# A four-layer residual kernel: where the first batch's weight splits sit, with four raw tiles and nine ring places in place of two and ten

## The chip, the cores and the metric

The kernel runs on one core of one Trainium2 chip. Its time is the device time of one execution in microseconds (us); the figure for a kernel is the median of its runs.

## The reference

Sixteen batches of a 256 x 256 input go through four residual layers, each `x = x + layer(x)`.

- Layer 0: a causal moving average along the sequence, a gate from `x` and that average, then 16 further gated moving averages ("traces"), mixed with per-batch weights, a second gate, a projection and a layer norm.
- Layer 1: `p = softmax(mask + v . tanh(x W1 + b1))` over 256 positions, then `pooled = p x / count`.
- Layer 2: eight experts and one shared expert, each `(silu(x Wg) * (x Wu)) Wd` with hidden width 1024, added up with per-batch gate values. All nine sets of weights are used for every batch.
- Layer 3: `gelu(x W1 + b1)` of width 1024, then an output of 192 shared columns and 64 columns whose weights each batch picks from eight sets.

```python
g = einsum('bsd,edf->ebsf', h, Wg); u = einsum('bsd,edf->ebsf', h, Wu)
expert_outs = einsum('ebsf,efd->ebsd', silu(g) * u, Wd)
expert_output = einsum('be,ebsd->bsd', gating_probs, expert_outs)
```

## The kernel before

**Split operands.** Every big matmul is done three times: a float32 operand is split into a rounded high part (`rnd`, line 89, ScalarE) and a low part, the rest (`low`, line 96, a subtraction on VectorE or GpSimd), and `mm3` (lines 102 to 104) adds up high x high, high x low and low x high. Batch 0 alone takes layers 0 and 1 in plain float32 (`first_traces`, `first_pooled`), without splits.

**Weights.** Layer 2 has 72 weight pieces, here called chunks, of 128 x 768 floats, and `load_chunk` brings one in: a DMA from HBM into a raw tile (`raws`, two buffers), `rnd` on ScalarE into the high half of a ring tile (`ring`, `RING = 10` places), and `low` on GpSimd or VectorE into the other half. A raw tile is free again when `low` has read it; a ring place when TensorE has done the last matmul with the chunk. On the second visit the split chunk is stored in HBM (`keep`), and from then on it is loaded ready-made straight into its ring place, without a raw tile. Layer 3 has eight chunks `w_f` and four `w_c` for each pair of batches, in the same ring. `prefetch(n)` issues the next n chunks of a fixed list; behind each work item as many are issued as chunks are done with.

**Order of the work.** Layer 2 is a list of units. `l2_unit` makes up to 512 columns of `pg` and `pu`, `hidden` makes `silu(pg) * pu` and splits it (`hh`), and `down` multiplies by `Wd` into `y`, two units later (`LAG = 2`). For the first five experts (`ALONE`) batch 0 rides alone: 20 units of two chunks each. From unit 21 on batches 0 and 1 ride together, one chunk to a unit; further pairs join later (batches 2 and 3 at unit 57). In between, the steps of layers 0 and 1 of the next batches (`traces(b)`, `pooled(b)`) are dealt out by `pace`, so that a batch is ready when it boards. `issue_after(ins)` puts the instructions of a block that run on the engine of `ins` behind it in that engine's queue, and does nothing to those on other engines. Within these limits a scheduler decides the order on every engine, and each engine runs its queue strictly in order.

**What the change touches.** The small weights of layers 0 and 1 (`small_a`, `small_b`) are split by `split_small` into `wh` and `wl`: three pieces behind the first batch's traces, and four (`rest`) at steps 1, 6, 9 and 12 of batch 1's traces in program order. Eight chunks of the first expert are prefetched around the first batch: which engine takes their low part is decided in `load_chunk`:

```python
if kind == "e" and key[1] == 0:
    e = "g" if key[2] < 2 else "v" if key[2] < 6 else "gv"[key[2] % 2]
elif kind == "e" and key[1] < ALONE and key[2] % 3 == 0:
    e = "g"
```

In `first_pooled`, `evict(c, ...)` copies PSUM tiles to SBUF, on ScalarE for `c = 0` and on VectorE otherwise.

Of the kernel before, what the change touches and what calls it, by code (L numbers as in the profile page):

```python
# [11 lines left out]
AF = mybir.ActivationFunctionType  # L12
ALU = mybir.AluOpType
# [4 lines left out]
S = 256  # L18
# [1 line left out]
ND = 16  # L20
NE = 8
NF = 8
RING = 10
FRONT = 4
FRONT0 = 3
SLACK = 16
# [8 lines left out]
FIRST = 13  # L35
# [4 lines left out]
O_N1, O_G, O_SO, O_TE, O_OU, O_W1, W_COLS = 0, 256, 1280, 1792, 2304, 2816, 3072  # L40

V_BG, V_BN1, V_BN2, V_BSO, V_BTE, V_B1, V_V, V_L3B1, V_B2, V_WN2, V_COLS = 0, 2, 3, 4, 6, 8, 9, 10, 18, 19, 67
# [3 lines left out]
def fused_kernel(  # L46
# [21 lines left out]
    V, G, A, PE = nc.vector, nc.gpsimd, nc.scalar, nc.tensor  # L68
# [2 lines left out]
    xin = ctx.enter_context(tc.tile_pool(name="xin", bufs=2))  # L71
    l0 = ctx.enter_context(tc.tile_pool(name="l0", bufs=1))
    ring = ctx.enter_context(tc.tile_pool(name="ring", bufs=RING))
    raws = ctx.enter_context(tc.tile_pool(name="raws", bufs=2))
    xs = ctx.enter_context(tc.tile_pool(name="xs", bufs=3))
    accp = ctx.enter_context(tc.tile_pool(name="accp", bufs=3))
    hp = ctx.enter_context(tc.tile_pool(name="hp", bufs=2))
# [7 lines left out]
    last_of = {}  # L85
# [51 lines left out]
    def split_small(c0, n, e):  # L137
        rnd("a", wh[:, c0 : c0 + n], small(c0, n))
        low(e, wl[:, c0 : c0 + n], small(c0, n), wh[:, c0 : c0 + n])
# [6 lines left out]
    vec = const([P, V_COLS], F32, "vec", vecs)  # L146
# [42 lines left out]
    mhalf = cp.tile([P, 2], F32, name="mhalf")  # L189
# [69 lines left out]
    rest = {1: (O_SO, 512), 6: (O_TE, 512), 9: (O_OU, 512), 12: (O_W1, 256)}  # L259

    def traces(b):

        xr = xin_tiles.pop(b)
        xh, xl = hl(f"x_{b}", "hA")
        rnd("a", xh, xr)
        low("g", xl, xr, xh)
        cx = ft("ta", f"ctx{b}")
        for c in range(2):
            V.tensor_tensor_scan(
                cx[:, c], decay[:, ND : ND + 1].to_broadcast([P, S]), xr[:, c], 0.0, ALU.mult, ALU.add  # L270
            )
        yield
        ch, cl = hl(f"c_{b}", "hA")
        rnd("a", ch, cx)
        low("v", cl, cx, ch)

        ph = ps_l.tile([P, 512], F32, tag="ps", name=f"ph{b}")
        for k in range(2):
            o = O_N1 + k * P
            mm3(ph[:, :S], W(0, o, P), W(1, o, P), xh[:, k], xl[:, k], k == 0, k == 1)  # L280
        hg = l0.tile([P, S], F32, tag="hg", name=f"hg{b}")
        A.activation(hg, ph[:, :S], AF.Gelu, bias=vec[:, V_BN1 : V_BN1 + 1])
        hs = l0.tile([P, S], F32R, tag="hs", name=f"hs{b}")
        rnd("a", hs, hg)
        low("v", hs[64:], hg[64:], hs[64:])
        yield
        pm = ps_l.tile([P, 512], F32, tag="ps", name=f"pm{b}")
        PE.matmul(pm[:48, :S], n2[:, 0], hs, start=True, stop=False)
        PE.matmul(pm[:48, :S], n2[:, 1], hs, start=False, stop=True)
        md = l0.tile([48, S], F32, tag="md", name=f"md{b}")  # L290
        A.activation(md, pm[:48, :S], AF.Tanh, bias=hb[:48, V_BN2 : V_BN2 + 1], scale=0.5)
        V.tensor_scalar(md, md, 0.5, 1.0, ALU.mult, ALU.add)
        mdd = dram.tile([1, ND, S], F32, tag="mdd", name=f"mdd{b}")
        nc.sync.dma_start(mdd[0], md[0:ND])
        yield
        pg = ps_l.tile([P, 2, S], F32, tag="ps", name=f"pg{b}")

        ga = ps_a.tile([P, 2, S], F32, tag="ga", name=f"gp{b}")
        for m in range(2):
            for k in range(4):  # L300
                o = O_G + k * S + m * P
                xa, xb_ = (xh[:, k], xl[:, k]) if k < 2 else (ch[:, k - 2], cl[:, k - 2])
                mm3(pg[:, m], W(0, o, P), W(1, o, P), xa, xb_, k == 0, k == 3)
        for m in range(2):
            A.activation(ga[:, m], pg[:, m], AF.Tanh, bias=hb[:, V_BG + m : V_BG + m + 1], scale=0.5)
        V.scalar_tensor_tensor(ga, ga, 1.0, xr, ALU.add, ALU.mult)
        yield
        sm = ft("sm", f"sm{b}")

        def soma():  # L310
            pso = ps_l.tile([P, 2, S], F32, tag="ps", name=f"pso{b}")
            for m in range(2):
                for k in range(2):
                    o = O_SO + k * S + m * P
                    mm3(pso[:, m], W(0, o, P), W(1, o, P), xh[:, k], xl[:, k], k == 0, k == 1)
            for m in range(2):
                A.activation(sm[:, m], pso[:, m], AF.Gelu, bias=vec[:, V_BSO + m : V_BSO + m + 1])

        tacc = ft("ta", f"ta{b}")
        for d in range(ND):  # L320
            if d % 2 == 0:
                mod = l0.tile([P, 2, S], F32, tag="mod", name=f"mod{b}_{d}", bufs=2)
                nc.sync.dma_start(mod, mdd[0, d : d + 2].partition_broadcast(P))
            bt = ft("bt", f"bt{b}_{d}", 3)
            tr = tacc if d == 0 else ft("tr", f"tr{b}_{d}", 3)
            with tc.issue_after(last_of[0].ins) if b == 1 and "h" not in last_of else nullcontext():
                for c in range(2):
                    V.scalar_tensor_tensor(
                        bt[:, c], ga[:, c], bl[:, c, d : d + 1], mod[:, d % 2], ALU.mult, ALU.mult
                    )  # L330
            for c in range(2):
                V.tensor_tensor_scan(  # L332
                    tr[:, c], decay[:, d : d + 1].to_broadcast([P, S]), bt[:, c], 0.0, ALU.mult, ALU.add
                )
            if d:
                G.tensor_tensor(tacc, tacc, tr, ALU.add)  # L336
            if b == 1 and d in rest:
                split_small(*rest[d], "g")
            if d == 5:
                soma()  # L340
            yield
        th, tl = hl(f"t_{b}", "hA")
        rnd("a", th, tacc)
        low("v", tl, tacc, th)
        xt = xt_tiles.pop(b)
        G.tensor_tensor(xt, xt, bet.unsqueeze(1).to_broadcast([P, 2, S]), ALU.add)
        held[b] = xt, sm, th, tl
        yield
# [122 lines left out]
    def evict(c, o, i):  # L471

        if c == 0:
            last_of["ca"] = A.activation(o, i, AF.Copy)
        else:
            last_of["cv"] = V.tensor_copy(o, i)
# [83 lines left out]
    def first_pooled():  # L560
# [19 lines left out]
        rs = l0.tile([P, 2], F32, tag="rs", name="rs0")  # L580
# [5 lines left out]
            V.bn_stats(st[:, t], po[t])  # L586
            V.bn_aggr(mv[:, t], st[:, t])
        V.tensor_scalar(rs, mv[:, :, 1], 4e-5, None, ALU.add)
        G.tensor_tensor(rs, rs, mhalf, ALU.pow)
        for t in range(2):  # L590
            V.scalar_tensor_tensor(po[t], po[t], mv[:, t, 0:1], gam, ALU.subtract, ALU.mult)
        yield
# [6 lines left out]
        ptr = two("ptr0")  # L599
# [2 lines left out]
                PE.transpose(ptr[c][:, t * P : (t + 1) * P], x1[:, t, c * P : (c + 1) * P], ident)  # L602
        x1T = ft("xo", "x1T0")
        for c in range(2):
            evict(c, x1T[:, c], ptr[c])
        yield
        pa = ps_l.tile([P, 512], F32, tag="ps", name="pa0")
        for k in range(2):
            PE.matmul(pa[:, :S], small(O_W1 + k * P, P), x1T[:, k], start=k == 0, stop=k == 1)
        ta = l0.tile([P, S], F32, tag="th", name="th0")  # L610
        last_of["ca"] = A.activation(ta, pa[:, :S], AF.Tanh, bias=vec[:, V_B1 : V_B1 + 1])
        yield
        psc = ps_l.tile([P, 512], F32, tag="ps", name="psc0")
        PE.matmul(psc[:, :S], vec[0:64, V_V : V_V + 1].to_broadcast([64, P]), ta[0:64], start=True, stop=True)
# [12 lines left out]
        for j in range(2):  # L627
            js = slice(j, j + 1)
            V.tensor_tensor(sums[:, js], sums[:, js], cntb[:, 0, js], ALU.mult)
            V.reciprocal(sums[:, js], sums[:, js])  # L630
            last_of["cv"] = V.tensor_scalar(sc[:, j], sc[:, j], sums[:, js], None, ALU.mult)
        yield
        ppt = two("ppt0")
        for l in range(2):
# [1 line left out]
                PE.transpose(ppt[l][:, j * P : (j + 1) * P], sc[:, j, l * P : (l + 1) * P], ident)  # L636
        q = ft("bt", "q0", 3)
        for l in range(2):
            evict(l, q[:, l], ppt[l])
        yield  # L640
        pp = two("pp0")
        for l in range(2):
# [17 lines left out]
    def load_chunk(key):  # L660
# [10 lines left out]
        if kind == "e":  # L671
            n = 768
# [14 lines left out]
        e = "v"  # L687
        if kind == "e" and key[1] == 0:

            e = "g" if key[2] < 2 else "v" if key[2] < 6 else "gv"[key[2] % 2]  # L690
        elif kind == "e" and key[1] < ALONE and key[2] % 3 == 0:
            e = "g"
        low(e, t[:, 1, :n], raw[:, :n], t[:, 0, :n])
# [181 lines left out]
    def prefetch(n, boost=BOOST):  # L875
        while n > 0 and nxt[0] < len(order):
            k = order[nxt[0]]
            if k[0] == "c" and k[1] not in eregs:
                eregs[k[1]] = nc.sync.value_load(eix[0:1, k[1] : k[1] + 1], min_val=0, max_val=NE - 1)
            with tc.high_priority(offset=boost) if boost else nullcontext():  # L880
                load_chunk(k)
            nxt[0] += 1
            n -= 1
# [61 lines left out]
            with tc.issue_after(last_of["cx"].ins):  # L945
                later_constants()
    with tc.issue_after(last_of["a"].ins), tc.issue_after(last_of["g"].ins), tc.issue_after(last_of["tr"].ins):
        for off, n in ((O_N1, 256), (O_G, 512), (O_G + 512, 512)):
            split_small(off, n, "g")
        prefetch(2, 0)  # L950


    n = 2
    while n_done[0] < 1:
        with tc.issue_after(last_of["ca"].ins), tc.issue_after(last_of["cv"].ins):
            next(steps)
            if n_steps[0] > FIRST + 5 and n < 6 and n_steps[0] % 2:
                prefetch(1, 0)
                n += 1
    with tc.issue_after(last_of["ca"].ins), tc.issue_after(last_of["cv"].ins):  # L960
        coefs()
        prefetch(RING - n)
# [155 lines left out]
```

## Time and profile before

| what | value |
|---|---|
| median of 3 runs (lowest to highest) | 2840.18 us (2839.82 to 2841.34) |
| profiled execution: its own time / its span | 2841.92 us / 2840.2 us |
| mean granted TensorE clock of it | 0.994 |
| TensorE matmul busy / VectorE / ScalarE / GpSimd | 98% / 50% / 43% / 46% |
| HBM read / written | 304.62 MB / 64.21 MB, 130 GB/s |

In the profile PE is TensorE's matmuls, PEld its weight loads, DVE VectorE, ACT ScalarE, POOL GpSimd, and SP the queue that issues nearly all DMAs. Durations of matmuls are modelled and overlap, so a busy PE is not one at its peak; counts of matmuls say more. Where two numbers stand at the front of a line of the timeline, they are its start and its length in us.

### The profile page before, as it was taken

The page shows a single profiled execution, that of the slowest core. Times are in us where ns is not written, and L with a number is a line of the kernel's source. Part 1 is how long each engine was busy: PE and PEld are TensorE (multiplying, and loading weights), DVE is VectorE, ACT ScalarE, POOL GpSimd, SP SyncE. Part 2 cuts the span into 40 slices and gives each one's busy share as a digit, 9 for nine tenths or more (in the row PEclk, how much of TensorE's full clock was granted, in tenths as well). Part 3 has the DMA queues.
Part 4 walks back from the last instruction along what each step waited for, and adds up shares of the span by engine and source line. Part 5 has one row for each costly group of instructions (what it writes and reads, how often), then busy time and mean ns, then how long its engine had stood idle before and what let it go on. Part 6 is the DMA issues. An engine that isn't in the chain of part 4 may idle for free. (4 is left out here: it accounts for less than half of the span.)

```text
span 2840.2 us, 36878 instructions
## 1 busy us (share of the span) xinstructions
PE 2779.2 (98%) x13604; PEld 2335.0 (82%) x13604; DVE 1425.2 (50%) x2646; ACT 1235.4 (43%) x2043; POOL 1299.0 (46%) x986
## 2 busy tenths in 40 slices
PE   7889989999999999999999999999999999999998
PEld 4877779888888888888888888888888888888887
DVE  7888766665665364544545445453444542222222
ACT  5555544546444533435334443334433453323433
POOL 5764654544544353544534445444444443333333
PEclk9999999999999999999999999999999999999999
DMA  4444645546443533324433153331523242222552
GB/s 125 136 148 122 196 162 181 185 131 230 148 164 117 180 115 104 119 77 135 150 110 106 40 180 112 111 117 58 177 101 112 91 169 90 89 89 76 192 198 83
DMA packets 114693, 371.23 MB, mean 131 GB/s; under 512 B 12642, under 2 KB 30930, under 8 KB 114514
## 3 DMA queue, kind: packets, MB, share of 16 engines
q1 hardware_dynamic: 114082, 368.82, 39.2%
q8 instruction: 108, 1.77, 0.3%
q14 instruction: 71, 0.58, 0.1%
q10 hardware_dynamic: 432, 0.06, 0.0%
HBM read 304.62 MB, written 64.21 MB: 130 GB/s over the span
## 5 line engine op out<-in xcount | busy, mean ns | idle before, releaser
L96 POOL TENSOR_TENSOR hh<-h,hh 128x512 fp32r<-128x512 f32 x640 | 848.7, 1326 | 1317.4 <-ACT hh L89 1297.4
L745 DVE TENSOR_TENSOR h<-h,pu 128x512 f32<-128x512 f32 x576 | 393.5, 683 | 941.9 <-PE pu L104 813.0
L89 ACT ACTIVATE hh<-h 128x512 fp32r<-128x512 f32 x640 | 403.4, 631 | 936.0 <-DVE h L745 914.9
L744 ACT ACTIVATE h<-pg 128x512 f32<-128x512 f32 x576 | 342.8, 595 | 317.7 <-PE pg L104 236.5
L102 PE MATMUL pg<-x,w_e 128*128 128x512 f32 (+1 forms) x1232 | 466.3, 379 | 10.1 <-ACT h L744 3.9
L102 PE MATMUL pu<-x,w_e 128*128 128x512 f32 (+1 forms) x1232 | 464.9, 377 | 7.5 <-ACT h L744 7.4
L104 PE MATMUL pg<-x,w_e 128*128 128x512 f32 (+1 forms) x1232 | 465.3, 378 | 1.8 <-DVE w_e L96 1.4
L103 PE MATMUL y<-hh,w_e 128*128 128x512 f32 (+1 forms) x1232 | 463.7, 377 | 2.5 <-POOL hh L96 2.5
L103 PE MATMUL pg<-x,w_e 128*128 128x512 f32 (+1 forms) x1232 | 464.7, 377 | 0.8 <-POOL x L96 0.8
L103 PE MATMUL pu<-x,w_e 128*128 128x512 f32 (+1 forms) x1232 | 463.7, 376 | 0.0
L104 PE MATMUL pu<-x,w_e 128*128 128x512 f32 (+1 forms) x1232 | 463.7, 376 | 0.0
L104 PE MATMUL y<-hh,w_e 128*128 128x512 f32 (+1 forms) x1232 | 463.1, 376 | 0.0
L102 PE MATMUL y<-hh,w_e 128*128 128x512 f32 (+1 forms) x1232 | 415.2, 377 | 2.9 <-ACT hh L89 1.6
L336 POOL TENSOR_TENSOR ta<-ta,tr 128x512 f32<-128x512 f32 x225 | 308.9, 1373 | 84.4 <-DVE tr L332 72.1
L332 DVE TENSOR_TENSOR_SCAN tr<-decay,bt 128x256 f32<-128x256 f32 x450 | 284.7, 669 | 0.0
L102 PEld LDWEIGHTS pg<-x,w_e 128*128 128x128 f32 x1232 | 232.5, 189 | 53.1 <-ACT h L744 4.8
L102 PEld LDWEIGHTS pu<-x,w_e 128*128 128x128 f32 x1232 | 232.6, 189 | 51.2 <-ACT h L744 9.9
L103 PEld LDWEIGHTS y<-hh,w_e 128*128 128x128 f32 x1232 | 232.8, 189 | 46.3 <-POOL hh L96 4.6
L104 PEld LDWEIGHTS pg<-x,w_e 128*128 128x128 f32 x1232 | 232.7, 189 | 44.9 <-DVE w_e L96 2.4
L102 PEld LDWEIGHTS y<-hh,w_e 128*128 128x128 f32 x1232 | 231.5, 189 | 45.7 <-ACT hh L89 2.6
L104 PEld LDWEIGHTS y<-hh,w_e 128*128 128x128 f32 x1232 | 232.7, 189 | 41.8
L104 PEld LDWEIGHTS pu<-x,w_e 128*128 128x128 f32 x1232 | 232.5, 189 | 41.9
(279 smaller groups left out, 3220.8 us busy)
## 6 DMA issues: line engine op xcount, KB each, us to landing
w_e<-keep_e SPq DMA_DIRECT2D x216, 768.0 KB, 4.4
raw_e<-in_wexp_dram SPq DMA_DIRECT2D x144, 384.0 KB, 4.3
keep_e<-w_e SPq DMA_DIRECT2D x72, 768.0 KB, 4.3
mod<-mdd SPq DMA_DIRECT2D x120, 256.0 KB, 3.7
w_f<-keep_f SPq DMA_DIRECT2D x56, 384.0 KB, 3.5
raw_c<-in_comb_dram SPq DMA_DIRECT2D x32, 260.0 KB, 2.8
xr<-in_xT_dram SPq DMA_DIRECT2D x16, 256.0 KB, 3.7
xt<-in_x_dram SPq DMA_DIRECT2D x16, 256.0 KB, 2.7
```

Source lines behind the costliest of these rows:

```text
L89: last_of["ca"] = A.activation(out_, in_, AF.Copy)
L96: i = (V if e == "v" else G).tensor_tensor(out_, in_, h.bitcast(F32), ALU.subtract)
L102: PE.matmul(o, wh, xh, start=start, stop=False, **kw)
L103: PE.matmul(o, wh, xl, start=False, stop=False, **kw)
L104: last_of["pe"] = PE.matmul(o, wl, xh, start=False, stop=stop, **kw)
L332: V.tensor_tensor_scan(tr[:, c], decay[:, d : d + 1].to_broadcast([P, S]), bt[:, c], 0.0, ALU.mult, ALU.add)
L336: G.tensor_tensor(tacc, tacc, tr, ALU.add)
L744: A.activation(h, ps_g, AF.Silu)
L745: last_of["h"] = V.tensor_tensor(h, h, ps_u, ALU.mult)
```

## The change

- `raws` has four buffers, and `RING` is 9.
- Prefetches around the first batch are tied to other instructions: chunks 0 and 1 of the first expert are issued between the pieces of the small weights, 2 and 3 behind the `rs` power of `first_pooled` on GpSimd and the last ScalarE step, 4 behind its tanh, 5 behind its softmax division; the rest, three and not four, after the batch.
- The low parts of the first six chunks go to engines v, g, g, g, v, v (before: g, g, v, v, v, v), where v is VectorE and g GpSimd.
- `x1T` and `q` of `first_pooled` are copied from PSUM by ScalarE alone.
- The four `rest` splits of the small weights stand in an `issue_after` block on the low part of batch 0's `x2`.

```diff
-RING = 10
+RING = 9
-    raws = ctx.enter_context(tc.tile_pool(name="raws", bufs=2))
+    raws = ctx.enter_context(tc.tile_pool(name="raws", bufs=4))
...
             if b == 1 and d in rest:
-                split_small(*rest[d], "g")
+                with tc.issue_after(last_of[0].ins):
+                    split_small(*rest[d], "g")
...
-        G.tensor_tensor(rs, rs, mhalf, ALU.pow)
+        last_of["rs"] = G.tensor_tensor(rs, rs, mhalf, ALU.pow)
...
-            evict(c, x1T[:, c], ptr[c])
+            evict(0, x1T[:, c], ptr[c])
...
-            evict(l, q[:, l], ppt[l])
+            evict(0, q[:, l], ppt[l])
...
-            e = "g" if key[2] < 2 else "v" if key[2] < 6 else "gv"[key[2] % 2]
+            e = "vgggvv"[key[2]] if key[2] < 6 else "gv"[key[2] % 2]
...
-        for off, n in ((O_N1, 256), (O_G, 512), (O_G + 512, 512)):
+        prefetch(1, 0)
+        split_small(O_N1, 256, "g")
+        prefetch(1, 0)
+        for off, n in ((O_G, 512), (O_G + 512, 512)):
             split_small(off, n, "g")
-        prefetch(2, 0)
...
             next(steps)
-            if n_steps[0] > FIRST + 5 and n < 6 and n_steps[0] % 2:
+        if n == 2 and "rs" in last_of:
+            with tc.issue_after(last_of["rs"].ins), tc.issue_after(last_of["ca"].ins):
+                prefetch(2, 0)
+            n += 2
+        if n == 4 and "th" in last_of:
+            with tc.issue_after(last_of["th"].ins):
                 prefetch(1, 0)
-                n += 1
+            n += 1
+        if n == 5 and "sc" in last_of:
+            with tc.issue_after(last_of["sc"].ins), tc.issue_after(last_of["ca"].ins):
+                prefetch(1, 0)
+            n += 1
```

More of the change, by code (lines that the diff above doesn't have):

```diff
@@ L610, in first_pooled @@
         ta = l0.tile([P, S], F32, tag="th", name="th0")
-        last_of["ca"] = A.activation(ta, pa[:, :S], AF.Tanh, bias=vec[:, V_B1 : V_B1 + 1])
+        last_of["ca"] = last_of["th"] = A.activation(ta, pa[:, :S], AF.Tanh, bias=vec[:, V_B1 : V_B1 + 1])
         yield
@@ L630, in first_pooled @@
             V.reciprocal(sums[:, js], sums[:, js])
-            last_of["cv"] = V.tensor_scalar(sc[:, j], sc[:, j], sums[:, js], None, ALU.mult)
+            last_of["cv"] = last_of["sc"] = V.tensor_scalar(sc[:, j], sc[:, j], sums[:, js], None, ALU.mult)
         yield
```

## The prediction, made before the changed kernel was run

> **What bounds the kernel now.** I read the page's busy rows first, then the stretches of the first 400 us, then who waited for whom there, then single instructions.
>
> ```profile
> span 2840.2 us, 36878 instructions
> PE 2779.2 (98%) x13604; PEld 2335.0 (82%) x13604; DVE 1425.2 (50%) x2646; ACT 1235.4 (43%) x2043; POOL 1299.0 (46%) x986
> ```
>
> TensorE is the bound. Its count of matmuls does not change (the built kernel's queues hold the same matmuls), so only lost time can move. A run of 256-column matmuls starts one every 0.118 us (60 to 80 us: 169 in 20 us), 512-column ones every 0.213 us (1000 to 1500 us: 2352 in 500 us, no idle time). From 1000 to 2000 us nothing is to be had. The stretches before are another matter:
>
> ```profile
> core 0: us, PE busy (x) PEld busy (x) DVE busy (x) ACT busy (x) POOL busy (x), PEclk, DMA share, GB/s
> 78.00:101.00 23.00, 19.56 (x144) 18.65 (x143) 23.00 (x42) 10.19 (x16) 17.74 (x12) 0.93 0.49 153
> 101.00:122.00 21.00, 17.62 (x122) 16.04 (x121) 16.95 (x29) 9.29 (x14) 20.69 (x14) 0.93 0.42 132
> 122.00:150.00 28.00, 26.10 (x211) 25.45 (x211) 22.44 (x31) 21.02 (x35) 18.28 (x13) 0.99 0.45 132
> 150.00:187.00 37.00, 28.82 (x220) 26.66 (x220) 26.32 (x48) 22.17 (x36) 15.98 (x11) 1.00 0.51 157
> 187.00:388.00 201.00, 182.86 (x920) 152.63 (x921) 160.51 (x284) 107.47 (x175) 107.62 (x76) 0.96 0.47 146
> ```
>
> From 78 to 187 us, batch 0 riding alone, there are 697 matmuls, 82 us of work in 109 us: 27 us are lost. From 78 to 122 us VectorE and then GpSimd is full (batch 1's traces); from 122 to 187 us no engine is. There the weights are late:
>
> ```profile
> ACT w_e L89 <- DMA raw_e<-in_wexp_dram: 28.5, 22, 4.1
> PEld pu L102 <- ACT h L744: 6.2, 5, 2.0
> PE pu L102 <- ACT h L744: 5.2, 4, 1.8
> PE pg L102 <- ACT w_e L89: 3.1, 2, 2.1
> ```
>
> ScalarE stood 28.5 us before roundings whose raw tile had not landed, and what is queued behind them (`h`, `hh`) stood too. One turn of one of the two raw tiles, in order of time:
>
> ```profile
> 118.67 1.09 DVE L96 TENSOR_TENSOR w_e<-raw_e,w_e 128x768 fp32r<-128x768 f32 x1 [2.24 <-ACT w_e L89]
> ...
> 124.04 0.83 ACT L89 ACTIVATE w_e<-raw_e 128x768 fp32r<-128x768 f32 x1
> ...
> 125.65 2.31 POOL L96 TENSOR_TENSOR w_e<-raw_e,w_e 128x768 fp32r<-128x768 f32 x1
> ```
>
> The low part that ends at 119.76 us frees the tile, the next DMA is issued at 119.78, its rounding runs at 124.04, its low part ends at 127.96, and at 127.99 comes the DMA after it: 8.2 us for one chunk through one of two tiles. Over 77.9 to 181.0 us 32 chunks were issued, one per 3.3 us; a unit needs two per 36 matmuls (4.25 us). So two raw tiles pace this part.
>
> **The change, part by part.** *First batch (36 to 59 us): 0, from -0.5 to +0.5.* `x1T`'s second half leaves VectorE, where it began at 47.81 behind three other operations though its matmuls ended at 46.35; ScalarE, no longer rounding chunk 3 there (0.83 us from 46.25), can do both halves by 47.2, up to 0.5 us before `pa` reads the second now. But chunk 4's rounding now follows the tanh, and its low part (0.96) stands on VectorE ahead of the `mx` reductions: the tanh from 49.0, 0.47 long, then 0.83 and 0.96, is 51.3, and `mx` begins at 51.33 now. The gain is spent. The low parts of chunks 2 and 3 on GpSimd (1.85 each, against 0.95) lie where it was idle (44.94 to 48.71), and their matmuls come at 59 us or later. The DMAs of chunks 2 and 3 (41.18 now) can go at about 15 us, ahead of nothing urgent on SP's queue.
>
> A low part on VectorE takes 0.95 us when GpSimd is still and up to 2.11 us when both run (60.78 us). The Trainium skill ("SBUF — State Buffer", "SBUF: two separate sides") says why: GpSimd and a VectorE operation with two SBUF inputs share a port pair, and the later one waits for the whole instruction. That speaks against the move to GpSimd; by it the low part of `c` could wait until 48.7 us for chunk 3's, and the term would still be 0, since `mx` waits for chunk 4.
>
> *The `rest` splits: 0.* The instruction they are tied to is VectorE's, the splits run on ScalarE and GpSimd, and in the built kernel's queues they stand where they stood (9.09 to 13.7 us on GpSimd). This part does not do what it says.
>
> *Four raw tiles, batch 0 alone (59 to 187 us): -3.0, from -8.8 to +4.* The new queue order shows what the scheduler makes of it. Counted from unit 1's first matmul (58.9 us), batch 1's `pt`, which needs the end of its traces, stands behind 496 matmuls, not 438; `psc` behind 788, not 660; unit 21 behind 852, not 840. Units run ahead of batch 1, and its last steps, spread over units 17 to 20 now, come in one piece after them. So:
> - `pt` starts at 124.66 now. The traces end on a GpSimd that is full, and one more `hh` (1.3) and one more low part (1.85) stand before that end: 124.7 + 3.2 = 127.9.
> - From `pt` to `psc` 292 matmuls: 34.5 us at 0.118, 39.9 at the 0.1365 of that stretch now (222 in 30.3 us, 124.66 to 154.96). I take the middle, 37.1, since the weights come sooner but a ring place comes later: 165.0.
> - From `psc` to unit 21 the serial piece. Batch 3 shows its price today:
>
> ```profile
> 369.05 0.38 PE L420 MATMUL psc<-ths,vr 128*128 128x256 f32 x1 [0.56 <-ACT md L291]
> 372.24 1.16 PE L445 MATMUL ppt<-ident,sc 128*128 128x128 f32 x4 [2.69 <-DVE sc L437]
> 375.30 0.55 PE L102 MATMUL pg<-x,wh 128*128 128x256 f32 x1 [1.90 <-DVE q L96]
> 380.89 0.38 PE L457 MATMUL pp<-q,v 128*128 128x256 f32 x1 [1.02 <-ACT gp L305]
> 385.34 0.50 PE L102 MATMUL pso<-x,wh 128*128 128x256 f32 x1 [2.76 <-DVE acc L461]
> 387.99 0.63 PE L102 MATMUL pg<-x,w_e 128*128 128x512 f32 x1
> ```
>
> 369.05 to 387.99 is 18.9 us for 54 matmuls (6.4 us of work). Unit 21 then runs from 165.0 + 18.9 = 183.9; now it runs freely from 186.9: -3.0. With GpSimd's 3.2 hidden and full rate it is 178.1 (-8.8); with nine ring places making each of some 14 units wait another 0.5 us it is +4 or so. (Matmuls in that piece run 0.21 us apart from 375.65 to 378.4, half speed, after gaps of 2.97 and 1.9 us.)
>
> The skill ("TensorE: Matmul & The Clock Gate", "What's actually happening") puts the half clock after an idle window of about 3.4 us. No single gap here is that long, so by the rule read gap by gap the piece would cost some 2.5 us less (an estimate from that page); the row shows the half speed, and the sum keeps the row.
>
> *Later gains from it (187 to 388 us): -4.6, from -8 to 0.* VectorE is full from 184 to 220 us (36.00 of 36) and from 260 to 300 (40.00 of 40). In the new order six more chunks are split before unit 21, so 6 x 1.13 us of low parts leave this stretch; about half of it lies where VectorE is the limit: -3.4. And 10 matmuls of unit 56 now stand between batch 3's `psc` and `ppt`, inside the 2.69 us wait: -1.2.
>
> *Nine ring places in layer 3: +1, from 0 to +7.4.* In steady layer 2 a chunk is loaded over 20 us before its use, and a place less costs nothing. In layer 3's eight blocks the ring turns faster:
>
> ```profile
> 2660.77 5.02 SPq L666 DMA_DIRECT2D w_f<-keep_f  x3
> 2666.98 9.02 SPq L666 DMA_DIRECT2D w_e<-keep_e  x6
> ```
>
> Each load goes when a place comes free: 2660.8, 2664.2, 2664.8, then 2667.0, 2672.6. With nine, each takes the next one's time. `w_f` 5 then lands at 2664.2 + 3.5 (the page's median) = 2667.7, and its matmul stands at 2667.49; the first `w_e` at 2672.6 + 4.4 = 2677.0, with its matmul at 2674.76. The same sum over all eight blocks gives 7.4 us of late landings (2.7 of it in the last block). But the new order moves just these matmuls back, here behind 15 to 18 `down` matmuls (over 3 us), which have to be done anyway; so I take +1.
>
> **The sum.** 0 - 3.0 - 4.6 + 1 = -6.6 us. The profiled execution would go from 2841.92 to 2835.3; it lies 1.7 above the median of the runs, 2840.18, which becomes 2833.6.
>
> **Rivals.** *The gain is eaten (0.30).* `pt` to `psc` stays at 0.1365 us a matmul because ring places and not raw tiles pace it, so unit 21 starts at 186.7 (-0.2); VectorE's relief finds TensorE busy; what is left is -1.2 + 1: 2839.8. For it: no engine but TensorE gains idle time before 122 us, and the new serial piece costs 12 us of idle TensorE. Against: the 28.5 us that ScalarE waits for raw tiles.
>
> *Slower: nine places are one too few (0.17).* The scheduler's idea of a DMA's time need not be the chip's; if the reordering doesn't cover the late landings, the eight blocks cost 7.4 us, and with the first gain eaten the time is 2847.6. It decides as soon as `w_f` lands over 3 us later than its order assumes. For it: leads of 1.3 to 5 us now at the last three `w_f` of most blocks. Against: layer 3 shows almost no wait in this profile, and landings there keep near 3.5 us.
>
> **How the numbers follow.** My case has 0.53 with 2833.6; adding its best ends gives 2822.9, which I hold for unlikely together, so the range starts at 2826. Upwards it must take in the eaten gain and half of the slower rival: 2844. A measurement of this kernel tells about 0.2% (5.7 us) from no change. My case is mostly just over that line: faster 0.51, same 0.32, slower 0.17.
>
> **What would show it.** Right: ScalarE's wait for `raw_e` between 78 and 184 us falls from 28.5 to under 10 us; the serial piece from `psc` to unit 21 is seen as idle TensorE of about 10 us before unit 21, which starts at 181 to 186 us; unit 57 starts 5 to 10 us before 388; from there to the end both traces differ by under 3 us. Wrong: waits of `q`, `z` or `pg` for `w_f` or `w_e` DMAs in layer 3 of over 1 us each; or ScalarE's wait for raw tiles turned into one for TensorE (`w_e` rounding behind `y`) of the same size, with unit 21 at 187 us or later.

## The result, and the profile after

The changed kernel is slower, by 0.3%: median 2850.26 us (2848.88 to 2854.37) against 2841.65 us (2839.82 to 2843.0) for the kernel before on the same chips, a ratio of 1.0032 with a 95% interval of 1.0023 to 1.0041. The forecast was 2833.6 with a range of 2826 to 2844. The profiled execution took 2851.74 us, against 2841.92.

The page's first rows, after:

```profile
span 2849.8 us, 36887 instructions
PE 2782.1 (98%) x13604; PEld 2337.4 (82%) x13604; DVE 1450.6 (51%) x2643; ACT 1241.0 (44%) x2050; POOL 1299.4 (46%) x987
```

The same 13604 matmuls, 9.6 us more span. The same five stretches as in the prediction (per engine busy us and count, then the granted clock):

```profile
78.00:101.00 23.00, 21.00 (x174) 20.66 (x173) 23.00 (x42) 14.20 (x20) 20.91 (x14) 1.00 0.49 150
101.00:122.00 21.00, 16.83 (x132) 15.81 (x131) 21.00 (x34) 10.22 (x15) 20.48 (x13) 1.00 0.56 160
122.00:150.00 28.00, 25.45 (x210) 25.25 (x211) 26.22 (x28) 16.60 (x27) 22.35 (x14) 1.00 0.51 153
150.00:187.00 37.00, 26.34 (x204) 25.05 (x203) 27.00 (x45) 24.71 (x42) 15.48 (x11) 0.90 0.63 191
187.00:388.00 201.00, 182.99 (x910) 151.11 (x908) 163.08 (x280) 103.07 (x169) 103.46 (x76) 0.97 0.41 129
```

From 78 to 150 us TensorE starts 516 matmuls; before it was 477. Then it falls back: 204 against 220 up to 187 us (a matmul that lies across a border of two stretches counts in both). VectorE (third of the engines) is now full until 122 us. Who waited for whom between 78 and 184 us (us in all, times, longest); the first line is of the kernel before, the others are of the changed one:

```profile
ACT hh L89 <- DVE h L745: 6.9, 7, 1.4
...
ACT hh L89 <- DVE h L746: 27.5, 15, 3.7
...
PE ppt L446 <- DVE sc L438: 6.7, 1, 6.7
...
ACT w_e L89 <- PE y L104: 5.8, 5, 2.5
...
ACT w_e L89 <- DMA raw_e<-in_wexp_dram: 1.4, 2, 0.9
```

ScalarE's wait for raw tiles is gone (28.5 us before, 1.4 now), but its wait for VectorE's `h` grew from 6.9 to 27.5 us, and TensorE got one gap of 6.7 us ahead of `ppt`. Roundings behind `y`, which wait for a ring place, stand for 5.8 us. The longer wait for `h` isn't a loss by itself: it is 23.8 us in the run below that takes both losses out, and that run is as fast as the kernel before. Matched by their places in TensorE's queue, the first matmuls of these blocks moved as follows (us):

| block | before | after | later by |
|---|---|---|---|
| second part of `pt` of batch 0 | 38.95 | 43.73 | 4.8 |
| unit 1 | 58.9 | 66.3 | 7.4 |
| unit 20 | 173.2 | 166.2 | -7.0 |
| `pt`, batch 1 | 124.7 | 135.1 | 10.4 |
| `psc`, batch 1 | 155.0 | 174.6 | 19.6 |
| unit 21 | 183.8 | 198.7 | 14.9 |
| unit 57 | 388.0 | 400.8 | 12.8 |
| last `down` | 2834.2 | 2844.1 | 9.9 |

So two losses: 7.4 us ahead of unit 1, and 7.5 more at unit 21, though unit 20 had come 7 us early.

**The first loss.** VectorE, GpSimd and TensorE of the changed kernel around 40 us, in order of time (other lines left out):

```profile
36.37 1.27 POOL L557 TENSOR_TENSOR xt<-xt,bet 128x512 f32<-128x512 f32 x1
37.60 0.72 POOL L96 TENSOR_TENSOR wl<-small_a,wh 128x256 fp32r<-128x256 f32 x1
37.64 5.71 DVE L96 TENSOR_TENSOR w_e<-raw_e,w_e 128x768 fp32r<-128x768 f32 x1
38.28 1.80 POOL L96 TENSOR_TENSOR w_e<-raw_e,w_e 128x768 fp32r<-128x768 f32 x1
40.05 2.48 POOL L96 TENSOR_TENSOR wl<-small_a,wh 128x512 fp32r<-128x512 f32 x2
43.27 0.41 DVE L477 COPY t<-ta 128x256 f32<-128x256 f32 x1
43.73 1.22 PE L570 MATMUL pt0g<-t,small_b 128*128 128x256 f32 x2 [3.23 <-DVE t L477]
```

The low part of chunk 0, moved to VectorE, stands ahead of the copy `t`, which the rest of batch 0 needs. It takes 5.71 us instead of 0.95: it ends at 43.35, 0.82 us after GpSimd's run of operations without a pause (to 42.53). In the kernel before, GpSimd did this low part, and `t` was copied at 37.96:

```profile
36.23 3.16 POOL L96 TENSOR_TENSOR wl<-small_a,wh 128x256 fp32r<-128x256 f32 x3
37.96 0.42 DVE L476 COPY t<-ta 128x256 f32<-128x256 f32 x1 [1.63 <-ACT t L474]
39.35 3.57 POOL L96 TENSOR_TENSOR w_e<-raw_e,w_e 128x768 fp32r<-128x768 f32 x2
```

(1.4 us of the 5.3 lie ahead of this place: the first `pt` matmul stands at 39.38, before at 37.98; over the profiled executions below it lies between 37.9 and 39.3 with and without this edit.) TensorE then works at half speed as well: the mean granted clock from 44 to 50 us is 0.51, and was 0.79.

**The second loss.** TensorE from `psc` to unit 21, after (the first matmul of each step):

```profile
174.59 0.39 PE L421 MATMUL psc<-ths,vr 128*128 128x256 f32 x1 [0.59 <-ACT md L291]
182.96 1.17 PE L446 MATMUL ppt<-ident,sc 128*128 128x128 f32 x4 [6.66 <-DVE sc L438]
186.03 0.55 PE L102 MATMUL pg<-x,wh 128*128 128x256 f32 x1 [1.90 <-DVE q L96]
191.82 0.39 PE L458 MATMUL pp<-q,v 128*128 128x256 f32 x1 [1.02 <-ACT gp L305]
196.28 0.38 PE L102 MATMUL pso<-x,wh 128*128 128x256 f32 x1 [2.76 <-DVE acc L462]
198.71 0.63 PE L102 MATMUL pg<-x,w_e 128*128 128x512 f32 x1
```

The serial piece was forecast from batch 3's at 18.9 us and takes 24.1. The excess is all between `psc` and `ppt`: 8.4 us, against 3.2 in batch 3's. VectorE there, from the second half of that stretch (`...` marks left-out lines):

```profile
177.69 0.94 DVE L96 TENSOR_TENSOR w_e<-raw_e,w_e 128x768 fp32r<-128x768 f32 x1
...
178.95 0.94 DVE L96 TENSOR_TENSOR w_e<-raw_e,w_e 128x768 fp32r<-128x768 f32 x1
179.81 0.14 DVE L435 TENSOR_TENSOR sums<-sums,cntb 128x2 f32<-128x2 f32 x1
179.91 0.96 DVE L96 TENSOR_TENSOR w_e<-raw_e,w_e 128x768 fp32r<-128x768 f32 x1
180.79 0.16 DVE L436 RECIPROCAL sums<-sums 128x2 f32<-128x2 f32 x1
181.68 0.96 DVE L96 TENSOR_TENSOR w_e<-raw_e,w_e 128x768 fp32r<-128x768 f32 x1 [0.74 <-ACT w_e L89]
182.56 0.61 DVE L438 TENSOR_SCALAR sc<-sc,sums 128x256 f32<-128x256 f32 x2
```

Between the short steps of the softmax stand low parts of chunks 45 to 48, whose first matmuls come 41 us later and more; one more, of chunk 44, stands ahead of these lines. ScalarE is not free of them either: three roundings (2.30 us from 174.44) stand ahead of the exponentials, which start 3.5 us after `psc` (in batch 3's piece 1.3), and the last low part waited 0.74 us for its rounding. So "the splits" below are both, low parts and roundings.

### The profile page after: what moved, and what is told of

Read it like the earlier page. It is cut to its first block, busy times and chain, and to the rows that moved or that the text cites. A ratio compares the mean times of both kernels' runs of the same rounds, so it can differ in the third digit from the quotient of the medians.

```text
span 2849.8 us, 36887 instructions
## 1 busy us (share of the span) xinstructions
PE 2782.1 (98%) x13604; PEld 2337.4 (82%) x13604; DVE 1450.6 (51%) x2643; ACT 1241.0 (44%) x2050; POOL 1299.4 (46%) x987
## 4 chain that ended last, share of the span: by engine, by line
PE 88%; DVE 6%; issue 2%; ACT 1%; DMA 1%; POOL 0%; DVEq 0%; SPq 0%; ACTq 0%; POOLq 0%
PE pg L102 9%; PE pg L103 9%; PE pg L104 9%; PE pu L102 9%; PE pu L104 8%; PE pu L103 8%; PE y L104 8%; PE y L103 8%; PE y L102 8%; DVE tr L332 2%; DVE w_e L96 1%; DVE bt L328 1%; PE q L102 1%; PE q L103 1%; PE q L104 1%
```

## The experiments

Theory: the loss has these two places and no other. Rivals: other edits of the first batch; the ninth ring place; a chain that would be as long without the splits. Every kernel ran beside the kernel before; "over" is the difference of the two medians, the times of blocks are from the profiled execution, "end" is the last `down` against 2834.2 us. That one execution can lie some us off its kernel's median: e5's lies 3.4 us above, e14's 3.2 below. From unit 1 on, TensorE's order is that of the changed kernel in e1, e2, e5 and e7, and in e9 and e13 until past unit 21; e3 has that of the kernel before, and e14 that of e6 until past unit 21. The other runs have other orders, so what they show is the edit and what the scheduler made of it.

| run | over (us) | ratio, 95% interval | unit 1 | `psc` to `ppt` | `psc` to unit 21 | unit 21 | unit 57 | end |
|---|---|---|---|---|---|---|---|---|
| changed | +8.6 | 1.0023 to 1.0041 | 66.3 | 8.4 | 24.1 | 198.7 | 400.8 | +9.9 |
| e1_low0_pool | +4.4 | 1.0008 to 1.0026 | 59.7 | 9.6 | 25.3 | 193.7 | 393.3 | +2.6 |
| e2_old_first_4_9 | +2.6 | 1.0000 to 1.0019 | 58.5 | 8.7 | 24.2 | 191.4 | 392.8 | +2.1 |
| e3_first_only | +6.4 | 1.0014 to 1.0033 | 66.2 | 8.4 | 30.0 | 192.3 | 394.6 | +5.2 |
| e4_ring9 | +7.1 | 1.0018 to 1.0037 | 59.1 | 5.6 | 30.4 | 184.8 | 393.3 | +5.9 |
| e5_low01_dve | +8.0 | 1.0016 to 1.0036 | 64.0 | 8.5 | 24.1 | 198.2 | 402.2 | +11.3 |
| e6_raws4_ring10 | +0.3 | 0.9993 to 1.0011 | 58.0 | 7.3 | 23.0 | 189.4 | 392.1 | +1.2 |
| e7_low40_pool | +3.4 | 1.0002 to 1.0020 | 58.9 | 7.0 | 24.3 | 193.4 | 397.0 | +6.1 |
| e8_raws2_ring11 | +9.9 | 1.0024 to 1.0051 | 59.2 | 9.2 | 34.4 | 187.9 | 400.9 | +10.0 |
| e9_hold44 | -1.3 | 0.9986 to 1.0004 | 59.0 | 3.5 | 18.8 | 185.6 | 388.7 | -2.0 |
| e10_front3_9_4 | +3.3 | 1.0002 to 1.0020 | 60.0 | 8.2 | 20.1 | 193.6 | 392.1 | +7.0 |
| e11_front3_10_4 | +2.1 | 0.9998 to 1.0016 | 58.9 | 7.8 | 19.0 | 193.3 | 390.2 | -0.6 |
| e12_front3_10_2 | +5.6 | 1.0012 to 1.0030 | 60.4 | 6.2 | 26.9 | 185.5 | 394.7 | +8.1 |
| e13_both | +1.0 | 0.9994 to 1.0012 | 58.9 | 3.5 | 18.8 | 185.4 | 388.4 | -1.1 |
| e14_10_4_hold44 | +1.3 | 0.9994 to 1.0013 | 58.9 | 3.7 | 17.6 | 183.9 | 388.6 | -2.2 |

(With two raw tiles the way from `psc` to unit 21 is longer because units stand between the steps there; it is no serial piece.)

**Chunk 0's low part back on GpSimd.**

```diff
-            e = "vgggvv"[key[2]] if key[2] < 6 else "gv"[key[2] % 2]
+            e = "ggggvv"[key[2]] if key[2] < 6 else "gv"[key[2] % 2]
```

> The changed kernel with one edit: the low part of chunk 0 goes to GpSimd again (engines g, g, g, g, v, v). Theory A: the 7.4 us that unit 1 is late come from that one operation, which stood 5.71 us on VectorE ahead of the copy `t` while GpSimd ran without a pause. Then `t` is copied near 38.0 us again, unit 1 starts at 59 to 61 us instead of 66.3, and the median falls by 5.5 to 7.5 us, to some 2843 to 2845. Rival: the other edits of the first batch (chunks 2 and 3 on GpSimd, chunk 4 ahead of `mx`, both copies on ScalarE) make it late; then unit 1 stays at 64 us or later and the median falls by under 2 us. Second rival: the delay is taken up in the stretch in which batch 0 rides alone; then unit 1 is early and unit 21 and the end are not.

Measured: `t` is copied at 37.95, unit 1 starts at 59.7, and the lead of 6.6 us lasts: 7.3 us at the last `down`. Without the 1.4 us that already lay ahead of this place these are 5.2 and 5.9, and the medians say 4.2 (8.6 to 4.4), less than expected. One operation on the wrong engine is most of the first loss; with it back, unit 1 is within 0.8 us of the kernel before, and the median 1.8 us above the run with the old first batch, which the intervals do not separate.

**The sizes alone, the first batch alone, one size alone.**

```diff
-RING = 10
+RING = 9
-    raws = ctx.enter_context(tc.tile_pool(name="raws", bufs=2))
+    raws = ctx.enter_context(tc.tile_pool(name="raws", bufs=4))
```

> The kernel before with two numbers changed: four raw tiles, nine ring places; nothing of the first batch. TensorE's order is that of the changed kernel from unit 1 on. Theory B: running ahead costs more in the serial piece (`psc` of batch 1 to unit 21, 24.1 us measured) than it gains, whatever the first batch does: unit 1 at 59, unit 21 at 190 to 192 us, unit 57 at 392 to 395, layer 3 some 2.8 us shorter than before, median 2.0 to 4.0 us above the kernel before, 2843.5 to 2845.5. Rival (the prediction's sum, with only the first batch wrong): serial piece 19 us, unit 21 at 184, median 2835. Rival (the first batch's delay spoils the serial piece): serial piece under 21 us, median 2838 to 2841.

> The kernel before with the edits of the first batch alone; two raw tiles and ten ring places stay. Theory A: unit 1 at 66 us; with two raw tiles part of the delay is taken up, since chunks can be split while TensorE waits: unit 21 late by 3 to 7 us, median 3 to 7 us above the kernel before (2844.5 to 2848.5). Rival: the whole loss of the change is here: median 8 us above or more. Rival: raw tiles pace the stretch and take all of it up: median within 1.5 us of the kernel before.

> The kernel before with nine ring places instead of ten and nothing else. Theory C: layer 3 gets about 2.8 us shorter, as in the changed kernel, because the scheduler moves its matmuls back; the stretch to unit 57 changes by -2 to +4 us, since TensorE's order there changes too; median 2838.5 to 2843.5. Rival (the prediction's slower rival): nine places are too few, layer 3 gets up to 7.4 us longer, median up to 2849. Second rival: the shorter layer 3 belongs to the raw tiles; then it is as before.

Measured: the sizes alone give +2.6, with a serial piece of 24.2 us: theory B's numbers, and neither rival's. The first-batch edits alone give +6.4; unit 21 is 8.5 us late there, more than expected, and of the 7.3 us at unit 1, 5.2 are still there at the end. The two make 9.0 against 8.6 for the whole change. Nine places with two raw tiles is worse than with four: +7.1, against the expectation, and not in layer 3 (from unit 560 to the end 4.7 becomes 5.9), but between units 21 and 57 (4.3 us). Unit 20, too, is 5.8 us late, unit 21 only 1.0; batch 1's `pt` came early there (120.4). ScalarE still waits 22.4 us for raw tiles between 78 and 184 us (28.5 in the kernel before).

**What chunk 0's low part waits for.**

```diff
-            e = "vgggvv"[key[2]] if key[2] < 6 else "gv"[key[2] % 2]
+            e = "vvggvv"[key[2]] if key[2] < 6 else "gv"[key[2] % 2]
```

> The changed kernel with the low part of chunk 1 on VectorE too (v, v, g, g, v, v), right behind chunk 0's and ahead of the copy `t`. GpSimd's run without a pause gets shorter by that operation (1.80 us): `xt` 1.27, one `wl` 0.72, two `wl` 2.48, to about 40.8 us. If chunk 0's low part can only work when GpSimd's whole run is over, it lasts 3.0 to 3.6 us instead of 5.71, chunk 1's then 0.95, `t` is copied near 41.8 instead of 43.27, unit 1 starts near 65 and the median is 0.5 to 2 us below the changed kernel, though VectorE has more to do ahead of `t`. Rival: VectorE and GpSimd just slow each other, by a factor: chunk 0's low part lasts 5 us or more again, `t` comes at 44 us or later, unit 1 at 67 or later, the median 1 us or more above the changed kernel.

VectorE and GpSimd in this run (two low parts in the second line):

```profile
36.17 3.17 POOL L96 TENSOR_TENSOR wl<-small_a,wh 128x256 fp32r<-128x256 f32 x3
36.19 4.83 DVE L96 TENSOR_TENSOR w_e<-raw_e,w_e 128x768 fp32r<-128x768 f32 x2
40.95 0.41 DVE L477 COPY t<-ta 128x256 f32<-128x256 f32 x1
```

The first low part lasts 3.96 us (3.0 to 3.6 were expected) and ends at 40.15, 0.81 after GpSimd's run (39.34); the second takes 0.95. With twice the work on VectorE, `t` follows the start of the first low part by 4.76 us instead of 5.63. That is a wait for the run, and not a slowing by a factor. Unit 1 comes 2.3 us earlier (1.4 of them from the start), but unit 21 only 0.5 us, and the median is not clearly below the changed kernel's.

**Four raw tiles, and a ring place more.**

```diff
-    raws = ctx.enter_context(tc.tile_pool(name="raws", bufs=2))
+    raws = ctx.enter_context(tc.tile_pool(name="raws", bufs=4))
...
-        md = l0.tile([48, S], F32, tag="md", name=f"md{b}")
+        md = l0.tile([48, S], F32, tag="hg", name=f"md{b}")
...
-        x1T = ft("xo", f"x1T{b}")
+        x1T = ft("g2", f"x1T{b}")
```

(and the same for batch 0's tiles; the other run has RING = 11 instead)

> The kernel before with four raw tiles and all ten ring places; the 6 KB come from tiles that share a place with others that are dead by then (`ga0` and `x1T` with `sg`, `md` with `hg`). Nothing of the first batch. If the two sizes add up (nine places alone: +7.1; nine places and four raw tiles: +2.6), the four raw tiles alone bring -4.5: median 2835.5 to 2838.5, faster than both kernels. Rival: the serial piece ahead of unit 21 comes from running ahead, so from the raw tiles: unit 21 at 190 us or later as in the run with both sizes, and the median within 2 us of 2843. Second rival: the first stretch loses 7 us, the rest wins it back: median within 1.5 us of the kernel before.

> The kernel before with two raw tiles and eleven ring places (room as in the run with four raw tiles and ten places). If a ring place less costs 7.1 us because ready chunks lack a place, one more brings something too: median 2836 to 2840, with the gain between unit 1 and unit 57. Rival: the loss with nine places came from the order that the scheduler made of it and not from the place itself: then eleven places are as good as ten or worse, 2841 to 2846.

Measured: the two sizes do not add up. Four raw tiles with all ten places bring +0.3, not -4.5: unit 21 at 189.4, a little ahead of what the first rival gave, and the median fits it and the second rival alike. The run with an eleventh place is 9.9 us slower, beyond what its rival gave. So a place is not worth a fixed time in either direction; more likely it is the order that the scheduler makes of the first 400 us that counts, but no run shows that by itself. Both runs also let tiles share places, an edit that no run has alone; the first of them is at +0.3 with it. In the run with eleven places 8.8 us are lost between units 21 and 57; which instruction is to blame was not traced.

**The splits in the softmax, first to GpSimd, then held back** (both on the kernel with the old first batch, four raw tiles and nine places).

```diff
-        elif kind == "e" and key[1] < ALONE and key[2] % 3 == 0:
+        elif kind == "e" and (key[1] < ALONE and key[2] % 3 == 0 or key[1] == ALONE):
             e = "g"
```

> Four raw tiles, nine ring places, the first batch as before (that run: 2844.0), and the low parts of chunks 40 to 47 on GpSimd instead of VectorE. GpSimd has nearly nothing to do in the serial piece, and four low parts leave VectorE's queue from between the steps of batch 1's softmax. Theory B (low parts in that queue lengthen the piece): `psc` to unit 21 falls from 24.2 us to 20 to 22, unit 21 starts 2 to 4 us earlier, median 2840 to 2842.5. Rival: ScalarE's roundings, which stay, and the chain itself make the length: piece within 1 us of 24.2, median within 1 us of 2844. Second rival: GpSimd's low parts now lock VectorE's operations out: piece longer, median above 2845.

GpSimd, VectorE and TensorE in this run:

```profile
170.57 7.17 POOL L96 TENSOR_TENSOR w_e<-raw_e,w_e 128x768 fp32r<-128x768 f32 x4
172.77 1.42 DVE L434 TENSOR_TENSOR sums<-sums,cntb 128x2 f32<-128x2 f32 x1 [2.46 <-ACT sc L430]
174.96 2.93 DVE L437 TENSOR_SCALAR sc<-sc,sums 128x256 f32<-128x256 f32 x2
177.95 0.90 PE L445 MATMUL ppt<-ident,sc 128*128 128x128 f32 x3 [1.33 <-DVE sc L437]
```

The low parts have left VectorE's queue, and nothing is won: `psc` to `ppt` falls from 8.7 to 7.0 us, but the piece stays at 24.3, since the four `ppt` no longer come in one go. `sums` takes 1.42 us instead of 0.14, `sc` 2.93 instead of 0.61. The cost of the queue was exchanged for that of the lock, as VectorE's waiting for GpSimd's operations is called here; the roundings stayed. Only the next run separates the chain from both:

```diff
-        prefetch(len(done))
+        owing[0] += len(done)
+        if i < 20:
+            go = min(owing[0], max(44 - nxt[0], 0))
+            prefetch(go)
+        else:
+            go = owing[0]
+            with tc.issue_after(last_of["ca"].ins) if i == 20 else nullcontext():
+                with tc.issue_after(last_of["cv"].ins) if i == 20 else nullcontext():
+                    prefetch(go)
+        owing[0] -= go
```

> Four raw tiles, nine ring places, the first batch as before (that run: 2844.0), and chunks 44 to 49 are rounded and split only behind unit 21's `hh`: the five low parts and roundings that stood between the steps of batch 1's softmax are gone from VectorE's and ScalarE's queues, and GpSimd gets nothing in their place (in the run that gave them to GpSimd, its 7.2 us without a pause held VectorE's `sums` and `sc` up by 1.3 and 2.3 us). Theory: `psc` to `ppt` falls from 8.7 us to 3.2 to 4.2, as in batch 3's piece of the kernel before, the whole piece from 24.2 to 19 to 20, unit 21 starts at 186 to 188; since VectorE must make the low parts later, the end gains less: median 2840.5 to 2844. Rival: the piece is set by the chain itself and not by the splits: piece still 23 us or more, median 2844 or above.

```profile
169.47 0.16 DVE L434 TENSOR_TENSOR sums<-sums,cntb 128x2 f32<-128x2 f32 x1
169.67 0.17 DVE L435 RECIPROCAL sums<-sums 128x2 f32<-128x2 f32 x1
169.87 0.62 DVE L437 TENSOR_SCALAR sc<-sc,sums 128x256 f32<-128x256 f32 x2
170.28 0.81 PE L445 MATMUL ppt<-ident,sc 128*128 128x128 f32 x4 [1.82 <-DVE sc L437]
```

VectorE's softmax steps now follow each other. `psc` to `ppt` takes 3.5 us, the piece 18.8, what batch 3's row had promised, and unit 21 starts at 185.6. The end gains 4.1 us over the run with the splits in place (3.9 in the medians). Where the splits stand, low parts and roundings together, is the second loss.

**`pg` behind `pp`** (`FRONT = 3` in place of 4, on three pairs of sizes).

> Four raw tiles, nine ring places, the first batch as before, and FRONT 3 in place of 4: one step less of the next batch's traces (its `pg`, 24 matmuls) is dealt out beside `pooled` of batches 1, 3, 5 and so on, so `pg` stands behind `pp` and not ahead of it in TensorE's queue. If the serial piece is long because `pg` (5 us at half clock, and the gate behind it) stands ahead of `pp`, `ppt` to `pp` falls from 9.5 us to about 3, the piece from 24.2 to 16 to 18, unit 21 starts at 184 to 186, and the piece ahead of unit 57 gets shorter too: median 2832 to 2841. Rival: what `pg` leaves is lost later, since batch 2's and 4's traces start later and VectorE is full from unit 21 to unit 57: median 2842 to 2846.

> The same edit on four raw tiles and ten ring places (2842.4 without it, the kernel before 2842.1 beside it). Theory: the serial piece, 23.0 us there, falls to 15 to 17, median 2831 to 2839: faster than both kernels. Rival: given back between unit 21 and unit 57, median 2841 to 2845.

> The same edit on the kernel before (two raw tiles, ten ring places). Here no serial piece stands ahead of unit 21, units fill it; the gain is only ahead of unit 57 (18.9 us there, falling to 13 to 15): median 2836 to 2841. If the two sizes pay only once the serial piece is short, this one stays behind the run with four raw tiles by 2 us or more; rival: it is as fast or faster, and the raw tiles are worth nothing.

Measured: `ppt` to `pp` falls from 9.5 to 2.9 us, and with nine places and four raw tiles the piece from 24.2 to 20.1. But the new order brings `psc` 6.3 us later (173.5 against 167.2), so unit 21 comes later, not earlier. The medians say +3.3, +2.1 and +5.6: the rival's side on the first two. The third lies above its range and stays more than 2 us behind the two with four raw tiles, which its text had named as a possibility.

**Both losses taken out of the changed kernel; the same with ten places.** The two edits above (`"ggggvv"` and the held-back splits) on the changed kernel, and the held-back splits on four raw tiles and ten places.

> The changed kernel with both suspected losses taken away: chunk 0's low part on GpSimd, and chunks 44 to 49 held back behind unit 21's `hh`. If these two places are the whole cause, their gains add up (4.4 and 3.7 us in the medians, 7.3 and 4.1 in the profiles): median 2839 to 2842.5, no longer slower than the kernel before. Rival: something else of the change costs too (the other first-batch edits, the ninth place): median 2843.5 or above.

> Four raw tiles and ten ring places (the first batch as before, 2842.4 without this edit) with chunks 44 to 49 held back. If the splits in the softmax cost here what they cost with nine places, `psc` to `ppt` falls from 7.3 to 3.5 us, unit 21 starts near 185.5 and the median is 2837 to 2840: faster than both kernels by a little. Rival: the tenth place brings nothing once the piece is short: 2840 to 2842.

Measured: with both edits the changed kernel is at 1.0003 of the kernel before (0.9994 to 1.0012); 7.7 of its 8.6 us are gone. What is left cannot be told from nothing. The tenth place brings nothing once the piece is short: nearer the rival, with a profiled execution that ends 2.2 us earlier than before's, and a median 1.3 us above. No kernel of this study beats the kernel before by more than the measurement can tell.

## Why the prediction was wrong, step by step

- *First batch, forecast 0 (-0.5 to +0.5), measured +7.4 (6.0 without the start): one of the two steps that failed most.* The prediction named the lock between GpSimd and VectorE and weighed it for the low part of `c` beside chunk 3's. It never costed the one operation that the change moves the other way, chunk 0's low part onto VectorE ahead of `t`, next to GpSimd's busiest stretch (8.00 of 8 us from 36 to 44 us before). With that edit taken back the term is +0.8.
- *The lock's rule.* "SBUF — State Buffer", section "SBUF: two separate sides", in the Trainium skill says that whichever of the two starts first holds the shared ports for the whole instruction. By that, as an estimate, the low part would have waited for the `wl` in progress, 0.7 us. Measured is a wait for four operations in a row. Another low part of this size waited only for the operation in progress (last section).
- *`rest` splits, forecast 0.* Nothing in the traces speaks against it: with the sizes alone and without that edit, TensorE's order and the times to unit 21 are those of the changed kernel less the first batch.
- *Batch 0 alone, forecast -3.0.* Counted from unit 1, the traces' end came 3.0 us later (forecast 3.2): right. `pt` to `psc` took 39.5 us, inside the 34.5 to 39.9 given, against 37.1 taken. The serial piece took 24.1 instead of 18.9: the price came from batch 3, whose piece holds no splits, and the prediction counted the six more chunks split ahead of unit 21 only as a gain. Together +7.4 us on this term, which so becomes +4.4: the other step that failed most.
- *What is late next.* The raw tiles' wait fell from 28.5 to 1.4 us, as said, but VectorE's share of the stretch was taken as hidden. It was full at 78 to 101 us already, and now it is full to 122 us: from 101 to 122 us it has one low part more, and they take longer (five in 7.4 us against four in 4.4). Batch 1's traces and `h` are late instead. Unit 21 needs batch 1, so units that run ahead only wait there.
- *187 to 388 us, forecast -4.6, measured +1.0* (unit 21 at 198.7 is 11.8 after the 186.9 that the prediction counted from, unit 57 is 12.8 late). VectorE's relief did not show: from unit 21 to unit 57 it is busy for 163.4 us, before for 160.6 (from 186.9). Low parts did leave the stretch, 32 are there and not 39, but they take 43.0 us, as the 39 did (43.3): 1.34 us each in place of 1.11. What makes each longer was not traced. With the old first batch batch 3's piece, `psc` to unit 57, is 17.0 instead of 18.9 us; the -1.2 for that was about right, the -3.4 was not.
- *Nine places in layer 3, forecast +1 (0 to +7.4).* Inside its range. Between the runs with nine and ten places, both with four raw tiles and the old first batch, the last stretch from unit 560 differs by 0.6 us (with two raw tiles by 1.2), and the changed kernel's waits of TensorE for a DMA from 2520 us on (engine, what waited for what, us in all, times, longest) are only

```profile
PEld q L102 <- DMA w_f<-keep_f: 0.7, 2, 0.5
PE q L102 <- DMA w_f<-keep_f: 0.2, 1, 0.2
```

  The whole way from unit 57 to the end is 2.9 us shorter than before; runs with ten places and four raw tiles and with eleven places show 2.8, and nine places with two raw tiles show none of it, so it isn't the ninth place's. The run with the first-batch edits alone, whose sizes are those of before, is 1.4 us shorter there too, so about half of it may be chance. Why was not traced.

The terms measured, 7.4 + 4.4 + 1.0 - 2.9, make the 9.9 us of the last `down`. With both losses out (e13), unit 21 starts at 185.4, 1.5 us ahead of the 186.9, so half of the forecast -3.0 is there; unit 57, at 388.4 against 388.0, shows that the -4.6 isn't. The slower rival had the right sign and the wrong mechanism.

## What to carry to other kernels

Cost every moved operation at its new place, with what the other engine does in that very microsecond; a low part of 0.95 us in front of the critical copy cost some 5. Work that is not urgent does harm in a queue that holds a chain of short dependent steps: a buffer that lets it start earlier puts it there, and moving it to an engine that locks the chain out doesn't help; only holding it back did. And a stretch that ends when a chain is ready gains nothing from running ahead of that chain.

## What the runs showed of the hardware that was not expected

- A two-input VectorE operation of 128x768 that met a GpSimd run without pauses ended 0.82 us (changed kernel) and 0.81 us (two low parts on VectorE) after the whole run, not after the operation in progress. Not every operation of this size does: in the kernel before, the low part at 118.67 (shown in the prediction) ended at 119.76, 0.82 us after the GpSimd operation in progress (117.13 to 118.94), though the next (118.90 to 120.89) followed without a pause. In the run with low parts on GpSimd, short VectorE operations got in at a boundary too: `sums`, begun at 172.77, ended at 174.19, when the second of four GpSimd operations was over. What makes the difference stays open.
- One-input VectorE operations are held too: `sc` (a multiplication by a per-partition value) took 2.93 us for two beside GpSimd's low parts (the same run), 0.61 alone.
- TensorE ran all 24 matmuls of `pg` at half speed (0.21 us apart) in the run with the splits held back, after gaps of 1.82 and 1.90 us; neither is as long as the idle window of about 3.4 us that "TensorE: Matmul & The Clock Gate" ("What's actually happening") in the Trainium skill names.
